# Moving normalizations up the ScalarE queue, turning the first keys early, and mirroring a quarter of the first batch's attention

## The chip, the cores and the metric

The kernel runs on one core of a Trainium2 chip. The metric is the device time of one execution in microseconds (us), less is better. Engines are named as in the profile: PE is TensorE, ACT ScalarE, DVE VectorE, POOL GpSimd, and SP the engine that issues most DMAs. A line number such as L1052 is a line of the kernel before.

## The reference, cut to what matters

There are 16 batches of 1024 rows with 256 features, and per batch a symmetric 0/1 matrix adj of 1024 x 1024. Two layers follow each other; in both the input is normalized, cut at zero and given to a graph block, whose result is added to the input.

```python
# layer 0, for each batch; 8 heads of 32 features
normed = layer_norm(relu(norm(x)), gamma1, beta1)      # queries, keys and values are all this
scores = q @ k.T / sqrt(32); masked where adj == 0; attn = softmax(scores)
h = h + attn @ v
h = h + gelu(layer_norm(h, gamma2, beta2) @ W1 + b1) @ W2 + b2
x = x + h
# layer 1, for each batch
f = relu(norm(x))
logits = (f W a_1).T + f W a_2 + (f W a_12)(f W).T     # leaky relu, mask by adj, softmax
x = x + elu(f @ W_1 + softmax(logits) @ f @ W_2)
```

Queries and keys are one and the same and adj is symmetric, so the matrix of attention weights before the division is symmetric too. What was computed for keys 512 to 1023 against queries 0 to 511 is, turned over, what keys 0 to 511 against queries 512 to 1023 need. The kernel calls that quarter mirrored.

## The kernel before, in words

The program is unrolled over all 16 batches. It is made by several generators (stream_a for attention, stream_b for everything after it, stream_c for the start of a batch, stream_m for masks, stream_p and stream_s for preparations). Each yields a place on a common scale, where b to b+1 is the attention of batch b, and the one with the smallest place goes next. The order in which instructions are made is the order on each engine's queue; the queues are not reordered afterwards. An engine, and SP for its DMAs, works its queue strictly in that order and waits where an operand is missing.

`defer(us, f)` holds f back until an estimated clock has moved on by that much, and `run_deferred` runs what is due. `turns` holds jobs on PE that are let in between two units of attention.

Attention goes by units: one group g of four heads, one half qh of the queries (512) and one tile kt of 128 keys. `scores` (L1016) makes the logits in two PSUM tiles, DVE adds the mask (L1029) and ACT takes the exponential and sums it (L1036, "exps" below); one unit later `weigh` (L1131) multiplies by the values va into o. In batch 0 the first of the two tiles gets its mask on PE instead, by a product with the identity (L574, "s<-mk,ident").

From batch 1 on, the units of qh = 1 with kt below 4 are left out. For each unit of qh = 0 with kt of 4 or more, `mirror` does four things. DVE turns 32 x 32 blocks of the weights into a tile x (L1052, two halves); SP writes x to DRAM in four DMAs (blocks, L1059); POOL adds up x in six operations (add_up, L1065) to row; and SP writes row (L1080). `gather` reads the rows back as sums of the softmax, `fetch` reads blocks back as em (L1099, 512 KB each), and `weigh_mirrored` (L1113) multiplies em by va. The pool of x holds one buffer.

Batch 0 has nothing to run beside its attention: the products of the batch (pty, ph, po, ptf, puT, pg, lg, pa, pf on PE) of batch b run beside the attention of batch b+1, and pty is the first of them. In `prologue(b)`, rows are loaded as h in four chunks, normalized (POOL takes the power -0.5, L745), cut by ACT (L816), normalized again to nrm (DVE, L749), multiplied by gamma (POOL, L829) and increased by beta (L830) to va; PE turns va (ptk, L837) and ACT copies it to kT (L840), the keys. For batch 0 `convert` makes masks of adj and `dma_start_transpose` turns them (mk). For other masks, `turn_masks` loads adj in halves (L587, two buffers), converts them (DVE, L594) and turns them; `compare_masks` checks on POOL (odd, L932) that adj is symmetric.

`normalize_later` takes part in every batch: DVE makes a factor nm (L759) 3.0 estimated us after the statistics, and ACT applies it to y or ft (L765) 5.0 after. y goes to PE as pty, ft as ptf (L1367); ACT copies ptf to fT (L1370), which puT, pg and lg read.

Of the kernel before, what the change touches and what calls it, by code (L numbers as in the profile page):

```python
# [9 lines left out]
F32 = mybir.dt.float32  # L10
# [485 lines left out]
def fast_path(  # L496
# [129 lines left out]
    def weight(src, name, pad=0):  # L626
# [3 lines left out]
        return t  # L630

    g1 = broadcast_row(gamma1, "g1")
    be1 = broadcast_row(beta1, "be1")
    for t, src in rows_to_load:
        nc.scalar.dma_start(t, src)
    rows_to_load.clear()
# [118 lines left out]
    def normalize_later(dst, srcs, stats, name, function):  # L755
        mv, rs = stats
        nm = smallp.tile([P, TPC], F32, tag="nm2", name=f"nm_{name}")
        defer(
            3.0, lambda: nc.vector.scalar_tensor_tensor(nm, mv[:, :, 0], -1.0, rs, op0=ALU.mult, op1=ALU.mult)  # L759
        )  # L760

        def apply():
            t = dst()
            for i, src in enumerate(srcs):
                nc.scalar.activation(t[:, i, :], src, function, bias=nm[:, i : i + 1], scale=rs[:, i : i + 1])  # L765

        return defer(5.0, apply)

# [20 lines left out]
    def prologue(b, st):  # L789
# [33 lines left out]
        def value(i):  # L823
            mv, rs = stats["b", i]
            for j in range(TPC):
                t = i * TPC + j
                nrm = tmpp.tile([P, D], F32, tag="w1", bufs=6, name=f"nrm_{b}_{t}")
                normalize(nrm, h[t // TPH][:, t % TPH, :], mv, rs, j)
                nc.gpsimd.tensor_mul(nrm, nrm, g1)  # L829
                nc.gpsimd.tensor_add(va[:, t, :], nrm, be1)  # L830

        def turn(i):
# [18 lines left out]
        if b == 0:  # L851
# [20 lines left out]
            rectify(0)  # L872
            convert(0)
            rectify(1)
            measure(0, "b")
            convert(1)
            measure(1, "b")
            value(0)
            turn(0)
            convert(2)  # L880
            value(1)
            turn(1)
            convert(3)
# [86 lines left out]

    scored = []

# [17 lines left out]
    def attention(b, st):  # L990
        va, kT = st["va"], st["kT"]
        mirrored = b > 0
        sums = {}
# [6 lines left out]
        def scores(qh, g, kt):  # L1000
# [4 lines left out]

            by_pe = 2 if b == 0 else 0
            if by_pe:
# [37 lines left out]

        def mirror(g, kt, es):
            x = xp.tile([P, NT // 2 * GH, GH, HD], F32, tag="x", name=f"x_{b}_{g}_{kt}")
            if g not in blocks:
# [15 lines left out]
            def add_up():  # L1064
# [30 lines left out]
        def fetch(k):  # L1095
            g, t, half = k // (2 * TPH), k // 2 % TPH, k % 2
            if k == 0:
                blocks["e"] = midp.tile([P, 2, 2 * GH, P], F32, tag="mid0", name=f"em_{b}")
            nc.sync.dma_start(  # L1099
                blocks["e"][:, half],  # L1100
                blocks[g][half * 2 * GH : (half + 1) * 2 * GH, t * GH : (t + 1) * GH].rearrange(
                    "k b i e -> (b i) k e"
                ),
            )

        def weigh_mirrored(k):
            g, t, half = k // (2 * TPH), k // 2 % TPH, k % 2
            e = blocks["e"][:, half]
            if t == half == 0:
# [10 lines left out]
            clock[0] += 0.45  # L1120
            if k + 2 < 2 * TPH * NG:
                defer(0.6, lambda: fetch(k + 2))

        acc, os, rl = {}, {}, {}

        def weigh(qh, g, kt, es, first, last):
            if first and not (mirrored and qh == 1):
                acc[g, qh] = pso.tile([P, QW], F32, tag="o", name=f"o_{b}_{g}_{qh}")
            o = acc[g, qh]
            for j in range(GH):  # L1130
                nc.tensor.matmul(  # L1131
                    o[j * HD : (j + 1) * HD, :],
                    va[:, kt, (g * GH + j) * HD : (g * GH + j + 1) * HD],
                    es[j // 2][:, j % 2, :],
                    start=first and not (mirrored and qh == 1),
                    stop=last,
                )
# [9 lines left out]
        def invert(qh, g):  # L1147
            r = smallp.tile([P, TPH, GH], F32, tag="rl", name=f"rl_{b}_{g}_{qh}")

            def f():  # L1150
                if mirrored and qh == 0:
                    nc.vector.tensor_reduce(
# [9 lines left out]

            rl[g, qh] = r, defer(2.5 if mirrored and qh == 0 else 2.5, f)

        keys = list(range(NT))
        if mirrored:
            keys = [kt for pair in zip(keys[TPH:], keys[:TPH]) for kt in pair]
        units = [(0, g, kt) for g in range(NG) for kt in keys]
        keys = list(range(TPH if mirrored else 0, NT))
        units += [(1, g, kt) for g in range(NG) for kt in keys]  # L1170
        k = 0
        for n, u in enumerate(units):
# [7 lines left out]
            scored.append((weigh, (*u, es, first, last)))  # L1180
            if not mirrored:
                if qh == NQH - 1 and kt % TPH == TPH - 1:
                    invert(kt // TPH, g)
                    if kt < NT - 1:
                        close(kt // TPH, g)
                yield 1.0
                continue
            if qh == 0:
                if kt >= TPH:
                    mirror(g, kt, es)  # L1190
                if n == NG * NT - 3:
                    defer(2.0, lambda: fetch(0))
                    defer(2.2, lambda: fetch(1))
                if n == NT + 1:
                    gather(0)
                if n == NT + 3:
# [374 lines left out]
    def stream_a():  # L1571
        for b in range(B):
            done = 0.0
            yield b
            for width in attention(b, states[b]):
                done += width
                yield b + done / (WIDTH if b else NQH * NG * NT)
        yield from spread(close_attention(), 4, B, B + .1)
# [150 lines left out]
```

## Time and profile before

| | us |
|---|---|
| median of 3 runs | 3367.99 (3364.7 to 3368.45) |
| the profiled execution | 3366.83 |
| its span, first to last instruction | 3365.1 |
| PE busy in the span | 3249.6 (97%) |
| DVE busy | 2688.1 (80%) |
| ACT busy | 2123.7 (63%) |
| POOL busy | 1517.0 (45%) |
| mean granted clock of PE | 0.99 |

Busy time counts every moment in which an engine has an instruction in work. A line of the profile with several groups names the line of the kernel, engine, operation, what is written and read, how often, the busy time, the mean of one in ns, and the idle time ahead of it with what ended it. In a timeline the first number is the start in us from the start of the span, the second the duration; what stands in brackets is the idle time before it and what ended that. "xN" counts the instructions merged into a line.

### The profile page before, as it was taken

To read this page: it belongs to the slowest core of one execution; us is meant where nothing else is said; L and a number is where in the kernel's file an instruction comes from. 1 tells how busy PE (TensorE), PEld (TensorE's weight loads), DVE (VectorE), ACT (ScalarE), POOL (GpSimd) and SP (SyncE) were. 2 spreads that over 40 slices of the span, in tenths; PEclk is the share of its full clock that TensorE was granted. 3 is DMA by queue.
4 is the path that set the end of the run, shared out by engine and by line. 5 is a ranking of instruction groups with operands and counts; after the bars stand their busy time and mean duration, and the time that the engine had idled before them with its cause. 6 is when DMAs were issued, how large, how long until landed. Compare 5 with 4: busy or idle time off the path is not lost. (4 is left out here: it accounts for less than half of the span.)

```text
span 3365.1 us, 114909 instructions
## 1 busy us (share of the span) xinstructions
PE 3249.6 (97%) x48866; PEld 1602.6 (48%) x48866; DVE 2688.1 (80%) x5009; ACT 2123.7 (63%) x5128; POOL 1517.0 (45%) x1757
## 2 busy tenths in 40 slices
PE   6899999999999999999999999999999999999998
PEld 2244445444454544445444454444545444454477
DVE  5788888888888888887888888888888888878734
ACT  6775766757566576665756667576665756657442
POOL 3563553635436264452635536354362644525120
PEclk9999999999999999999999999999999999999999
DMA  5354555545555464554545546455554645553400
GB/s 137 69 123 126 132 124 136 128 123 135 120 133 126 120 138 123 129 123 134 127 126 130 126 134 128 126 131 121 129 125 124 140 116 136 118 136 92 125 30 14
DMA packets 741161, 404.83 MB, mean 120 GB/s; under 512 B 173216, under 2 KB 699936, under 8 KB 740640
## 3 DMA queue, kind: packets, MB, share of 16 engines
q1 hardware_dynamic: 740352, 397.14, 48.0%
q8 instruction: 386, 6.32, 0.8%
q14 instruction: 135, 1.11, 0.1%
q10 hardware_dynamic: 288, 0.26, 0.0%
HBM read 233.97 MB, written 146.54 MB: 113 GB/s over the span
## 5 line engine op out<-in xcount | busy, mean ns | idle before, releaser
L1036 ACT ACTIVATE e<-e 128x512 f32<-128x512 f32 x1504 | 928.3, 618 | 629.2 <-DVE e L1029 626.2
L1029 DVE TENSOR_TENSOR e<-s,mk 128x1024 f32<-128x1024 f32 x752 | 883.9, 1214 | 110.2 <-PE s L1016 100.9
L1016 PE MATMUL s<-kT 32*64 32x512 f32 x6272 | 464.2, 629 | 0.5 <-DVE e L1029 0.5
L574 PE MATMUL ph<-yT,w 128*32 128x256 f32 x7808 | 449.9, 381 | 12.9 <-DVE yT L1298 12.7
L574 PE MATMUL lg<-fT,uT 128*32 128x256 f32 x7680 | 450.3, 379 | 0.3 <-ACT gw L1397 0.3
L574 PE MATMUL pa<-gw,e 128*32 128x258 f32 x7584 | 446.1, 380 | 0.0
L1131 PE MATMUL o<-e,va 128*32 128x512 f32 x3136 | 435.8, 617 | 0.0
L574 PE MATMUL po<-w,hid 128*32 128x256 f32 x7680 | 434.5, 379 | 0.9 <-ACT hid L1326 0.9
L574 PEld LDWEIGHTS ph<-yT,w 128*32 128x32 f32 x7808 | 247.9, 110 | 223.5 <-DVE yT L1298 44.5
L574 PEld LDWEIGHTS po<-w,hid 128*32 128x32 f32 x7680 | 255.1, 110 | 198.6 <-issue 46.1
L574 PEld LDWEIGHTS lg<-fT,uT 128*32 128x32 f32 x7680 | 248.8, 110 | 198.2 <-issue 27.2
L574 PEld LDWEIGHTS pa<-gw,e 128*32 128x32 f32 x7584 | 246.2, 110 | 185.4 <-issue 22.1
L1052 DVE STREAM_TRANSPOSE x<-e 128x1024 f32<-128x1024 f32 x240 | 291.7, 1230 | 39.5 <-ACT e L1036 27.6
L1065 POOL TENSOR_TENSOR part<-part,x 128x512 f32<-128x512 f32 x240 | 311.2, 1297 | 18.8
L1421 ACT ACTIVATE e<-e,shift 128x512 f32<-128x512 f32 x256 | 183.2, 716 | 161.0 <-DVE e L1420 149.7
L1036 ACT ACTIVATION_READ_ACCUMULATOR e<-e 128x1 f32 x1504 | 281.0, 187 | 0.0
L932 POOL TENSOR_TENSOR odd<-mk,mq 128x512 bf16<-128x512 fp8e5 x192 | 219.4, 1160 | 132.2 <-DMA mk<-mq 132.2
L1415 DVE SCALAR_TENSOR_TENSOR e<-lg,gw,mk 128x256 f32<-128x256 f32 x512 | 223.4, 477 | 61.0 <-PE lg L574 49.7
L829 POOL TENSOR_TENSOR nrm<-nrm,g 128x256 f32<-128x256 f32 x128 | 100.5, 785 | 344.2 <-DVE nrm L749 344.2
L1065 POOL TENSOR_TENSOR part<-x 128x512 f32<-128x512 f32 x120 | 157.0, 1308 | 211.9 <-DVE x L1052 206.1
L745 POOL TENSOR_TENSOR rs_c<-ve_c,mhalf 128x2 f32<-128x2 f32 x64 | 44.6, 697 | 428.7 <-DVE ve_c L743 425.1
L1322 ACT ACTIVATE hid<-ph,b1c 128x256 f32<-128x256 f32 x512 | 202.3, 463 | 44.9 <-PE ph L574 30.4
(146 smaller groups left out, 4462.0 us busy)
## 6 DMA issues: line engine op xcount, KB each, us to landing
blocks<-x SPq DMA_DIRECT2D x480, 256.0 KB, 4.6
em<-blocks SPq DMA_DIRECT2D x240, 512.0 KB, 4.3
adj<-in_adj_dram SPq DMA_DIRECT2D x248, 256.0 KB, 3.6
h<-in_x_dram SPq DMA_DIRECT2D x64, 256.0 KB, 4.5
xb<-in_x_dram SPq DMA_DIRECT2D x128, 128.0 KB, 3.8
out_dram<-z SPq DMA_DIRECT2D x128, 128.0 KB, 4.1
rows<-row SPq DMA_DIRECT2D x120, 32.0 KB, 2.4
gather<-rows SPq DMA_DIRECT2D x120, 32.0 KB, 3.7
```

The costliest lines, as they stand in the source:

```text
L574: nc.tensor.matmul(out[c : c + HD], lhsT[:, c : c + HD], rhs, start=start, stop=stop)
L829: nc.gpsimd.tensor_mul(nrm, nrm, g1)
L932: nc.gpsimd.tensor_tensor(odd.rearrange("p (u v x) -> p u v x", u=2, v=2), key.rearrange("p (u v x) -> p u v x", u=2, v=2), query.rearrang ...
L1016: nc.tensor.matmul(sc[j // 2][c : c + P // 2, j % 2, :], kT[r, g, kt * P + c : kt * P + c + P // 2], kT[r, g, qs], start=j >= by_pe, stop= ...
L1029: nc.vector.tensor_tensor(e, masked, mb, op=ALU.add)
L1036: nc.scalar.activation(e[:, j], masked[:, j], AF.Exp, scale=SCALE, accum_out=sums[kt // TPH, g][:, n, kt % TPH, qh : qh + 1],)
L1052: nc.vector.transpose(x[:, :, 2 * i : 2 * i + 2, :].rearrange("p c h j -> p h c j"), es[i].rearrange("p h (c i) -> p h c i", i=HD),)
L1065: add = lambda out, p, q: nc.gpsimd.tensor_tensor(out, p, q, op=ALU.add)
L1131: nc.tensor.matmul(o[j * HD : (j + 1) * HD, :], va[:, kt, (g * GH + j) * HD : (g * GH + j + 1) * HD], es[j // 2][:, j % 2, :], start=first ...
L1322: nc.scalar.activation(hid[:, f0 + i, :], ph[:, i, :], AF.Identity, bias=b1c[:, f0 + i : f0 + i + 1])
L1415: nc.vector.scalar_tensor_tensor(e[:, j, :], lg[:, j, :], gw[:, kt, D : D + 1], st[c // 2][:, kt // 2, qs, kt % 2], op0=ALU.add, op1=ALU.add,)
L1421: ready = defer(2.5, lambda: nc.scalar.activation(e, e, AF.Exp, bias=shift))
```

## The change

`normalize_later` applies the factor 3.1 estimated us after the statistics instead of 5.0, in every batch.

For the first two chunks of batch 0, PE turns nrm itself, ahead of gamma and beta, and ACT applies both on the way to kT, where they are a scale and a bias for each partition (g1c, be1c). POOL makes va of it afterwards. The loads at the start stand in another order, and the parts of the prologue of batch 0 come at earlier places.

Batch 0 gets the mirrored quarter: its units with qh = 1 and kt below 4 are gone, those with qh = 0 and kt of 4 or more are mirrored, and its keys go in the order 0, 1, 4, 2, 5, 3, 6, 7 for the first group of heads and 4, 0, 5, 1, 6, 2, 7, 3 for the second. There em has four halves in two buffers, not two in one. The mask is put on by PE only for qh = 0. Since the estimated clock moves little between two units there, `mirror` runs what is left of the mirror before (mirror_done), and rows and gather are forced ahead too. The masks of batches 0 and 1 are turned at earlier places.

```diff
-        return defer(5.0, apply)
+        return defer(3.1, apply)
...
+                if b == 0 and i < 2:
+                    normed[t] = nrm
+                    continue
                 nc.gpsimd.tensor_mul(nrm, nrm, g1)
                 nc.gpsimd.tensor_add(va[:, t, :], nrm, be1)
+        def turn_normed(i):
...
+                    nc.tensor.transpose(
+                        pt[:, g, j * P : (j + 1) * P], normed[i * TPC + j][:, g * P : (g + 1) * P], ident
+                    )
+            for g in range(NG):
+                nc.scalar.activation(
+                    kT[:, g, i * CW : (i + 1) * CW], pt[:, g, :], AF.Identity, bias=be1c[:, g : g + 1], scale=g1c[:, g : g + 1]
+                )
+            for j in range(TPC):
+                t = i * TPC + j
+                nc.gpsimd.tensor_mul(va[:, t, :], normed[t], g1)
+                nc.gpsimd.tensor_add(va[:, t, :], va[:, t, :], be1)
...
-            for f, i in ((load, 0), (fetch, 0), (load, 1), (fetch, 1), (fetch, 2), (fetch, 3), (load, 2), (load, 3)):
-                f(i)
+            load(0)
+            load(1)
+            for t, src in first_rows:
+                nc.sync.dma_start(t, src)
+            for t in range(TPH):
+                fetch(t)
+            load(2)
+            load(3)
...
-            turn(0)
+            turn_normed(0)
...
-        mirrored = b > 0
+        ahead = 2 if b else 4
...
-            by_pe = 2 if b == 0 else 0
+            by_pe = 2 if b == 0 and qh == 0 else 0
...
         def mirror(g, kt, es):
+            run_deferred(mirror_done[0])
             x = xp.tile([P, NT // 2 * GH, GH, HD], F32, tag="x", name=f"x_{b}_{g}_{kt}")
...
+                mirror_done[1 + g] = clock[0] + 10.0
                 defer(10.0, lambda: nc.sync.dma_start(blocks["rows", g][kt - TPH], row.rearrange("p a t h -> p (a t h)")))
...
-            defer(6.5, add_up)
+            mirror_done[0] = defer(6.5, add_up)
...
-            if k == 0:
-                blocks["e"] = midp.tile([P, 2, 2 * GH, P], F32, tag="mid0", name=f"em_{b}")
+            if k < ahead and k % 2 == 0:
+                tag = "mid0" if b else f"mid{1 + k // 2}"
+                blocks["e", k // 2] = midp.tile([P, 2, 2 * GH, P], F32, tag=tag, name=f"em_{b}_{k // 2}")
...
+        keys = [[kt for pair in zip(range(TPH, NT), range(TPH)) for kt in pair]] * NG
+        if b == 0:
+            keys = [[0, 1, 4, 2, 5, 3, 6, 7], keys[1]]
+        units = [(0, g, kt) for g in range(NG) for kt in keys[g]]
+        units += [(1, g, kt) for g in range(NG) for kt in range(TPH, NT)]
...
                 if n == NG * NT - 3:
-                    defer(2.0, lambda: fetch(0))
-                    defer(2.2, lambda: fetch(1))
-                if n == NT + 1:
+                    for i in range(ahead):
+                        defer(2.0 + 0.2 * i, lambda i=i: fetch(i))
+                late = 0 if b else 2
+                if n == NT + 1 + late:
+                    run_deferred(mirror_done[1])
                     gather(0)
...
             if n == NG * NT + 1:
+                run_deferred(max(mirror_done))
+                run_deferred(max(mirror_done))
                 gather(1)
...
-                for place, _ in zip((0.02, 0.04, 0.07, 0.10, 0.13), prologue(b, states[b])):
+                for place, _ in zip((0.005, 0.01, 0.03, 0.07, 0.13), prologue(b, states[b])):
...
-                start, end = (b - 0.28, b - 0.10) if b == 1 else (b - 0.73, b - 0.60)
+                start, end = (b - 0.55, b - 0.40) if b == 1 else (b - 0.73, b - 0.60)
...
-                yield from spread(compare_masks(b, 0, states[b]), TPH, b + 0.02, b + 0.2)
-                yield from spread(turn_masks(b, 1, states[b]), 5, b + 0.23, b + 0.43)
-                yield from spread(compare_masks(b, 1, states[b]), 2 * TPH, b + 0.52, b + 0.7)
+                yield from spread(compare_masks(b, 0, states[b]), TPH, b + 0.02, b + 0.15)
+                yield from spread(turn_masks(b, 1, states[b]), 5, b + 0.17, b + 0.30)
+                yield from spread(compare_masks(b, 1, states[b]), 2 * TPH, b + 0.32, b + 0.42)
```

More of the change, by code (lines that the diff above doesn't have):

```diff
@@ L630, in weight @@
         return t
+    g1c = columns(gamma1, DC, "g1c")
+    be1c = columns(beta1, DC, "be1c")
+    for t, src in rows_to_load:
+        nc.scalar.dma_start(t, src)
+    rows_to_load.clear()
     g1 = broadcast_row(gamma1, "g1")
     be1 = broadcast_row(beta1, "be1")
-    for t, src in rows_to_load:
-        nc.scalar.dma_start(t, src)
+    first_rows = rows_to_load[:]
     rows_to_load.clear()
@@ L828, in value @@
                 normalize(nrm, h[t // TPH][:, t % TPH, :], mv, rs, j)
+                if b == 0 and i < 2:
+                    normed[t] = nrm
+                    continue
                 nc.gpsimd.tensor_mul(nrm, nrm, g1)
                 nc.gpsimd.tensor_add(va[:, t, :], nrm, be1)
+        normed = {}
+        def turn_normed(i):
+            clock[0] += 0.5
+            pt = ps_tile([P, NG, CW], f"ptk_{b}_{i}")
+            for g in range(NG):
[3 more added lines that the diff above has]
+                    )
+            for g in range(NG):
+                nc.scalar.activation(
+                    kT[:, g, i * CW : (i + 1) * CW], pt[:, g, :], AF.Identity, bias=be1c[:, g : g + 1], scale=g1c[:, g : g + 1]
+                )
+            for j in range(TPC):
+                t = i * TPC + j
+                nc.gpsimd.tensor_mul(va[:, t, :], normed[t], g1)
+                nc.gpsimd.tensor_add(va[:, t, :], va[:, t, :], be1)
         def turn(i):
@@ L872, in prologue @@
             rectify(0)
+            rectify(1)
             convert(0)
-            rectify(1)
             measure(0, "b")
-            convert(1)
             measure(1, "b")
             value(0)
-            turn(0)
+            turn_normed(0)
+            convert(1)
+            value(1)
+            turn_normed(1)
             convert(2)
-            value(1)
-            turn(1)
             convert(3)
@@ L967, in make_turns @@
             f()
-    scored = []
+    scored, mirror_done = [], [0.0, 0.0, 0.0]
     finished = {}
@@ L1096, in fetch @@
             g, t, half = k // (2 * TPH), k // 2 % TPH, k % 2
-            if k == 0:
-                blocks["e"] = midp.tile([P, 2, 2 * GH, P], F32, tag="mid0", name=f"em_{b}")
+            if k < ahead and k % 2 == 0:
+                tag = "mid0" if b else f"mid{1 + k // 2}"
+                blocks["e", k // 2] = midp.tile([P, 2, 2 * GH, P], F32, tag=tag, name=f"em_{b}_{k // 2}")
             nc.sync.dma_start(
-                blocks["e"][:, half],
+                blocks["e", k % ahead // 2][:, half],
                 blocks[g][half * 2 * GH : (half + 1) * 2 * GH, t * GH : (t + 1) * GH].rearrange(
@@ L1107, in weigh_mirrored @@
             g, t, half = k // (2 * TPH), k // 2 % TPH, k % 2
-            e = blocks["e"][:, half]
+            e = blocks["e", k % ahead // 2][:, half]
             if t == half == 0:
@@ L1120, in weigh_mirrored @@
             clock[0] += 0.45
-            if k + 2 < 2 * TPH * NG:
-                defer(0.6, lambda: fetch(k + 2))
+            if k + ahead < 2 * TPH * NG:
+                defer(0.6, lambda: fetch(k + ahead))
         acc, os, rl = {}, {}, {}
         def weigh(qh, g, kt, es, first, last):
-            if first and not (mirrored and qh == 1):
+            if first and qh == 0:
                 acc[g, qh] = pso.tile([P, QW], F32, tag="o", name=f"o_{b}_{g}_{qh}")
@@ L1134, in weigh @@
                     es[j // 2][:, j % 2, :],
-                    start=first and not (mirrored and qh == 1),
+                    start=first and qh == 0,
                     stop=last,
@@ L1150, in f @@
             def f():
-                if mirrored and qh == 0:
+                if qh == 0:
                     nc.vector.tensor_reduce(
@@ L1161, in f @@
                 nc.vector.reciprocal(r, r)
[L1163 to L1170, printed above, removed]
+            rl[g, qh] = r, defer(2.5, f)
+        keys = [[kt for pair in zip(range(TPH, NT), range(TPH)) for kt in pair]] * NG
[3 more added lines that the diff above has]
+        units += [(1, g, kt) for g in range(NG) for kt in range(TPH, NT)]
         k = 0
@@ L1180, in attention @@
             scored.append((weigh, (*u, es, first, last)))
[L1181 to L1187, printed above, removed]
             if qh == 0:
@@ L1191, in attention @@
                 if n == NG * NT - 3:
-                    defer(2.0, lambda: fetch(0))
-                    defer(2.2, lambda: fetch(1))
-                if n == NT + 1:
+                    for i in range(ahead):
[3 more added lines that the diff above has]
+                    run_deferred(mirror_done[1])
                     gather(0)
-                if n == NT + 3:
+                if n == NT + 3 + late:
                     invert(0, 0)
@@ L1576, in stream_a @@
                 done += width
-                yield b + done / (WIDTH if b else NQH * NG * NT)
+                yield b + done / WIDTH
         yield from spread(close_attention(), 4, B, B + .1)
```

## The prediction

> **What bounds the kernel now.** I read the busy time by stretches first: 0 to 20.9 us is the start, up to 138.8 the attention of batch 0 with nothing beside it, 500 to 1000 the repeating middle.
>
> ```profile
> core 0: us, PE busy (x) PEld busy (x) DVE busy (x) ACT busy (x) POOL busy (x), PEclk, DMA share, GB/s
> 0.00:20.90 20.90, 2.65 (x8) 1.36 (x8) 13.17 (x42) 4.25 (x7) 11.68 (x26) 1.00 0.70 194
> 20.90:60.00 39.10, 35.07 (x385) 9.18 (x388) 17.95 (x29) 32.49 (x100) 12.28 (x16) 1.00 0.42 113
> 60.00:100.00 40.00, 34.07 (x460) 10.10 (x453) 29.86 (x62) 32.77 (x104) 16.12 (x19) 1.00 0.30 77
> 100.00:138.80 38.80, 32.44 (x345) 8.65 (x343) 28.98 (x56) 28.71 (x88) 19.70 (x23) 1.00 0.39 83
> 500.00:1000.00 500.00, 491.87 (x7760) 239.84 (x7748) 415.98 (x766) 317.64 (x768) 224.28 (x257) 0.99 0.52 129
> ```
>
> In the middle PE works 98% of the time: there only a PE stall can be won. Batch 0's attention is a loop through PE, ACT and DVE in which none is full: 32 units in 118 us, 3.7 each; the timeline at 69.7, 72.8 and 75.9 has undisturbed units every 3.07. The first PE work of the next phase (pty) starts at 142.0.
>
> Next, PE's waits between 500 and 3100 us:
>
> ```profile
> PE ptf L1367 <- DVE mv_a L741: 21.7, 7, 3.8
> PE ptf L1367 <- ACT ft L765: 13.4, 5, 3.2
> ```
>
> Twelve waits of 2.9 in some 12.7 batches: one a batch, always before ptf. The timeline of one of them:
>
> ```profile
> 2075.79 0.57 ACT L1370 COPY fT<-ptf 128x512 f32<-128x512 f32 x1
> 2078.15 1.90 PE L574 MATMUL puT<-fT,wm 128*32 128x512 f32 x16
> 2082.71 1.07 ACT L765 ACTIVATE ft<-xb,nm_d,rs_d 128x256 f32<-128x256 f32 x2
> 2083.35 0.93 PE L1367 MATMUL ptf<-ident,ft 128*128 128x128 f32 x4 [2.71 <-ACT ft L765]
> ```
>
> ft is late because it stands behind four exps and an odd on ACT, though its factor nm_d was there at 2078.4. 12 of the 14 such stalls (batches 0 to 13) are followed by half a clock for 3.4 us or more (1.7 lost each).
>
> Last, the mirror of the later batches, since batch 0 gets it: its buffer x is single.
>
> ```profile
> blocks<-x SPq DMA_DIRECT2D x480, 256.0 KB, 4.6
> em<-blocks SPq DMA_DIRECT2D x240, 512.0 KB, 4.3
> ```
> ```profile
> 214.64 2.36 DVE L1052 STREAM_TRANSPOSE x<-e 128x1024 f32<-128x1024 f32 x2
> 221.20 3.86 SPq L1059 DMA_DIRECT2D blocks<-x  x4
> 231.28 1.25 DVE L1052 STREAM_TRANSPOSE x<-e 128x1024 f32<-128x1024 f32 x1 [4.36 <-DMA blocks<-x]
> ```
>
> The next turn waits, and all DVE with it, until the four writes have landed. The issues take 3.4 us where nothing holds SP; the last lands 2.6 + 4.6 = 7.2 after the first. Later batches have a mirror each 12 to 17 us, so this rarely shows.
>
> **What the skill says.** "TensorE: Matmul & The Clock Gate", Part 1, has a free-running window of 4096 cycles (3413 ns) that sets full or half rate. The trace agrees: half rate lasts 3.413 or 6.827 us, starts on that grid, and follows windows with 1.70 us idle or more (1.69 and 1.67 did not). "DMA: Bandwidth & Descriptors", Anatomy of one DMA, has semaphores waited for on the issuing sequencer, before dispatch; so a load behind a write that waits for DVE waits too. The trace agrees: SP's L587 waits 286.6 us for DVE's mq. "Perfetto Trace Analysis", Optimization Strategy, reads repeated bubbles as a possible lack of buffers; here the ptf bubble is queue order, the 4.36 above a buffer.
>
> **The change, part by part.** I took the built order of the changed program on each queue and set durations of this trace on it.
>
> *Start.* Both h loads go first, and the keys of chunks 0, 1 are turned from nrm, not from va: eight POOL products and sums (0.79 and 0.75) leave the path. Normalization done near 12.8 instead of 15.4, the last mask transposed near 17 (convert to 14.4, landing 2.5 after issue); first scores at 17 instead of 20.9: -3.9. Two activations a chunk replace one copy (2 x 0.46, from hid's row, for 0.58; beside the mask). It is given back: ptk_2 and ptk_3 now stand before units 1 and 4 and wait for va of chunks 2, 3, behind POOL (eight ops of 0.77, two pows of 0.7). By that walk unit 1 scores at 28.2 (26.2 before), the fourth mask ends near 37.6 (37.2 before). So 0; bounds -4 and +3. The gamma and beta loads moved to SP and ACT lie under the mask loads: 0, bounds 1.
>
> *Mirrored quarter.* Removed: 8 units at 3.07 = 24.6, and the mask by PE in 8 more (0.61 and a 0.42 gap each). Added on PE: 16 weigh_mirrored at 0.62; on DVE: 16 transposes at 1.23 and 8 masks at 1.22; on POOL: 8 add_ups of six ops, 5.3 (1.27 + 2 x 1.29 + 0.73 + 0.45 + 0.31); on SP: 32 writes, 16 em fetches, 8 rows, 8 gathers. The engines' sums allow a gain: DVE's 76.8 in the three stretches grows by 29.4 less 9.8 for the masks of lost units. The chain through x does not. The mirrored key tiles 4 to 7 of head group 0 I call x4 to x7, those of group 1 x14 to x17; each is turned in two halves by DVE. From one's first turn to the next one's:
> - x4 to x5: turn, mask, turn 4.7; adj_4 is behind the four writes on SP and lands 8.8 later, its second half 1.2 later, two converts 0.45; mask 1.2: **16.4**.
> - x5 to x6: adj_5 waits for the two adj buffers (3.6 after a convert): 6 to the second turn; adj_7 behind the writes and a transpose of 1.2, 9.3; two converts, mask: **17.7**.
> - x6 to x7: turns 2.5, writes landed 7.3: **9.9**; x7 to x14 with a mask and os between the turns: **11.8**.
> - x14 to x15: second turn at 5.7 (three reduces); h of batch 1 is loaded behind those writes, landing 9 later; stats 1.4, mask 1.2, reduces 2.7: **19.9**.
> - x15 to x16: second turn at 6.1, adj_1 behind the writes 8.6, converts, mask: **17.0**.
> - x16 to x17: second turn 4.4; adj_3 and four em fetches (1.37 an issue) stand before the writes, 5.8 to their issue, 7.2 to 9 to landing: **19.7**.
>
> Sum 112.4; from 37.6, x17 turns at 150.0. After it: second turn at +6.9, POOL's add_up of x17 behind ten POOL ops at +19.6, rows landed +22, gather issued +24; em of pairs 6, 7 stands behind that gather on SP and lands +30; five units of some 4 us follow, two em buffers sharing (4.3 a fetch and 2.7 issue): PE done at **+51**, 201 against 142.0: **+59**. Each wait has all units queued behind DVE, so none hides. Half clock in the gaps isn't counted (up to +8). Floor of it: seven spacings of 9.9 and 34 after = 141, -1.
>
> *mirror_done.* It only puts add_up, rows and gather earlier in the queues; counted above.
>
> *Apply at 3.1.* In each batch ft_0, ft_2, ft_3 and y_2 move up ACT's queue. ft_2 goes before the fT copy, waits there for nm_d (ACT blocked 2 us; the fT copy behind it, and puT on PE for that). puT then starts 1.75 after nm_d (activations 1.07, copy 0.57): over batches 0 to 13 a stall of 1.5 to 3.3, mean 2.3, for one of 2.95, and ptf takes 0.66, not 0.93: -0.95 a batch, -13. A window catches 1.7 idle in (3.41 - 2.3 + 1.2)/3.41 = 68%, for 12 of 14: -4. ft_0 waits 2 us ahead of the table load of 1.28; the exps start 0.3 later: +4. y_2, ft_3 find their factors ready; the hid and gw drains behind them come 1.1 later, PSUM of 3 covers it: 0, bounds 7 both ways. Sum **-13**, bounds -30 and +10.
>
> *Turning of batch 1's masks earlier* (POOL and SP work) is in the walk. The next phase starts with that work done: **-3**, bounds -8 and +3.
>
> Total 0 + 59 - 13 - 3 = +43 on an execution of 3366.8 (span 3365.1 and 1.7 around it; the median of the runs is 3368.0, 1.2 above): **3410**.
>
> **Rivals.** *A, the forecast:* x's single buffer and SP's order set batch 0's length; 3385 to 3440 with half to all of the extra waits; 0.68. *B, the chain near its floor (faster):* loads behind writes land in their shadow and x turns on the average each 9.9; -1 - 13 - 3 gives 3350. With 34 after, the total is 7 spacings - 86.4 against before (37.6 + 34 - 142.0 - 16): faster by 7 or more below 11.3 us a spacing. For it: engines' sums have room. Against it: only two of seven spacings in the order have no load or late stats between. 0.13. *C, half of the loads hidden:* spacing 12.5, 40 after: 165 against 142, less 16, +7: 3374; 0.12. *D, the exchange on ACT loses too:* clock halved in each batch still and exps late, ft_2 at +0.7 a batch: 59 + 10 - 3: 3433; 0.07. That the change doesn't do what it says is excluded by the built order. POOL as the bound: its 36 us from 42 to 138.8 and 42 of add_ups make 78, less than the 97 there.
>
> **Numbers.** 3410; from B's edge to D: 3358 to 3440. About 0.2% (7 us) can be told from no change. Faster: most of B, 0.13; within: 0.07; slower: 0.80.
>
> **What would show it.** In the changed profile: DVE's x turns waiting for blocks<-x and adj in batch 0, spacings of 10 to 20, pty near 200; one puT wait of some 2.3 a batch on fT in place of ptf's. Wrong if pty comes before 160, or DVE's waits for writes sum to under 20 us there; or if ptf still waits 3 us in the middle.

## The result, and the profile after

| | before | after |
|---|---|---|
| median of 4 runs each, us | 3368.22 | 3414.00 |
| ratio to before | | 1.013 [1.011, 1.015] |
| the profiled execution, us | 3366.83 | 3415.79 |
| its span, us | 3365.1 | 3414.0 |
| pty of batch 0 starts at, us | 142.0 | 209.6 |
| from there to the end of the span, us | 3223.1 | 3204.4 |

The change made the kernel slower by 46 us in the medians and by 49 in the profiled executions. The last two rows split that: batch 0's attention became 67.6 us longer, and all that follows became 18.7 us shorter. These two rows come from one execution of each kernel; the executions of the kernel before spread from 3359.6 to 3377.5 us, so a few us in them are not to be read. Line numbers are from here on those of the kernel that is shown; in the changed kernel L1085 turns x, L1092 writes blocks, L1148 is weigh_mirrored, L1061 adds the mask, L594 converts later masks, L744 takes the statistics of h, L763 makes nm, L769 applies, L1401 copies fT, L1428 gw.

Busy time by stretches in the changed kernel, with the columns of the table before. The fourth stretch runs to pty and is longer than before's.

```profile
20.90:60.00 39.10, 21.70 (x208) 5.25 (x208) 15.85 (x32) 19.40 (x58) 19.39 (x24) 0.86 0.52 131
60.00:100.00 40.00, 23.61 (x260) 7.13 (x260) 14.47 (x17) 12.32 (x42) 15.49 (x17) 0.71 0.62 131
100.00:138.80 38.80, 18.45 (x124) 4.20 (x124) 23.52 (x42) 12.95 (x39) 21.82 (x25) 0.68 0.54 126
138.80:209.60 70.80, 44.95 (x404) 13.86 (x400) 45.42 (x83) 33.13 (x100) 35.51 (x42) 0.79 0.74 183
500.00:1000.00 500.00, 487.86 (x7628) 236.74 (x7620) 421.83 (x790) 316.95 (x771) 237.91 (x274) 1.00 0.53 127
```

Read the first number in each group. Between 60 and 100 us PE is busy for 23.6 where it was 34.1, DVE for 14.5 where it was 29.9, ACT for 12.3 where it was 32.8; only POOL, which got the sums of x, has nearly as much to do as before. No engine is near full, so the question is what they wait for. DVE's longest waits for transfers, first in the kernel before up to 150 us, then in the changed one up to 220:

```profile
DVE mq L594 <- DMA adj<-in_adj_dram: 6.5, 6, 1.7
...
DVE st_a L740 <- DMA h<-in_x_dram: 3.6, 2, 2.0
```
```profile
DVE mq L594 <- DMA adj<-in_adj_dram: 26.1, 7, 9.2
DVE x L1085 <- DMA blocks<-x: 22.2, 3, 7.7
...
DVE st_a L744 <- DMA h<-in_x_dram: 9.1, 2, 7.2
```

The numbers are the sum in us, how often, and the longest. The three of the changed kernel make 57.4 us; before, the two make 10.1, and there are no writes of x to wait for. One such wait in the timeline, between the mirrors of x4 and x5: SP issues four writes from 48.80 and only then the adj loads, and DVE, which has the mask of the next unit queued behind the convert, stands for 9.15 us.

```profile
48.80 3.40 SPq L1092 DMA_DIRECT2D blocks<-x  x4
...
52.24 6.98 SPq L587 DMA_DIRECT2D adj<-in_adj_dram  x4
...
57.93 0.94 DVE L594 TENSOR_SCALAR mq<-adj 128x512 fp8e5<-128x512 int32 x2 [9.15 <-DMA adj<-in_adj_dram]
58.79 1.22 DVE L1061 TENSOR_TENSOR e<-s,mk 128x1024 f32<-128x1024 f32 x1
...
59.92 1.23 DVE L1085 STREAM_TRANSPOSE x<-e 128x1024 f32<-128x1024 f32 x1
```

In the middle (500 to 3100 us) PE's wait ahead of ptf is gone, and others stand in its place:

```profile
PE puT L574 <- ACT fT L1401: 22.1, 13, 3.1
PE pg L574 <- ACT gw L1428: 6.3, 12, 0.5
PE pg L574 <- ACT fT L1401: 6.1, 12, 0.5
```

In the timeline the order on ACT has turned round: ft now stands ahead of the copy to fT, both wait for nm_d, and puT waits for the copy.

```profile
2135.58 1.10 DVE L763 SCALAR_TENSOR_TENSOR nm_d<-mv_d,rs_d 128x2 f32<-128x2 f32 x1 [0.99 <-POOL rs_d L749]
...
2136.72 1.09 ACT L769 ACTIVATE ft<-xb,nm_d,rs_d 128x256 f32<-128x256 f32 x2 [1.71 <-DVE nm_d L763]
2137.72 0.56 ACT L1401 COPY fT<-ptf 128x512 f32<-128x512 f32 x1
...
2138.33 1.50 PE L574 MATMUL puT<-fT,wm 128*32 128x512 f32 x12 [1.74 <-ACT fT L1401]
```

Of the windows of half rate between 500 and 3100 us, 11 of 3.41 us in the kernel before, one is left.

### The profile page after: what moved, and what is told of

Same layout as the page of the kernel before. It is cut to its first block, busy times and chain, and to the rows that moved or that the text cites. A ratio compares the mean times of both kernels' runs of the same rounds, so it can differ in the third digit from the quotient of the medians.

```text
span 3414.0 us, 114649 instructions
## 1 busy us (share of the span) xinstructions
PE 3246.3 (95%) x48674; PEld 1610.6 (47%) x48674; DVE 2716.3 (80%) x5027; ACT 2110.7 (62%) x5066; POOL 1558.4 (46%) x1805
## 5 line engine op out<-in xcount | busy, mean ns | idle before, releaser
L1061 DVE TENSOR_TENSOR e<-s,mk 128x1024 f32<-128x1024 f32 x752 | 883.0, 1214 | 94.3 <-PE s L1048 89.0
L574 PE MATMUL ph<-yT,w 128*32 128x256 f32 x7808 | 454.9, 381 | 11.5 <-DVE yT L1329 11.4
L1166 PE MATMUL o<-e,va 128*32 128x512 f32 x3072 | 428.7, 613 | 0.0
L574 PEld LDWEIGHTS ph<-yT,w 128*32 128x32 f32 x7808 | 263.9, 110 | 206.1 <-DVE yT L1329 42.4
L1085 DVE STREAM_TRANSPOSE x<-e 128x1024 f32<-128x1024 f32 x256 | 311.4, 1230 | 54.1 <-ACT e L1068 27.3
L1098 POOL TENSOR_TENSOR part<-part,x 128x512 f32<-128x512 f32 x256 | 332.1, 1297 | 20.1
L574 PEld LDWEIGHTS pa<-gw,e 128*32 128x32 f32 x7584 | 246.2, 110 | 185.3 <-issue 22.1
L1098 POOL TENSOR_TENSOR part<-x 128x512 f32<-128x512 f32 x128 | 167.0, 1305 | 250.0 <-DVE x L1085 244.2
```

The source lines that it names most:

```text
L574: nc.tensor.matmul(out[c : c + HD], lhsT[:, c : c + HD], rhs, start=start, stop=stop)
L1061: nc.vector.tensor_tensor(e, masked, mb, op=ALU.add)
L1085: nc.vector.transpose(x[:, :, 2 * i : 2 * i + 2, :].rearrange("p c h j -> p h c j"), es[i].rearrange("p h (c i) -> p h c i", i=HD),)
L1098: add = lambda out, p, q: nc.gpsimd.tensor_tensor(out, p, q, op=ALU.add)
L1166: nc.tensor.matmul(o[j * HD : (j + 1) * HD, :], va[:, kt, (g * GH + j) * HD : (g * GH + j + 1) * HD], es[j // 2][:, j % 2, :], start=first ...
```

## The experiments

Each was timed against the kernel before on the same chip. The last column counts windows of half rate, 3.41 us each, between 500 and 3100 us in the trace's record of the granted clock. It and the two columns ahead of it are of the profiled execution alone. Where an expectation speaks of 12 windows in the middle of the kernel before, this count has 11.

| run | median us | before beside it | ratio to before | pty at | pty to end | half rate |
|---|---|---|---|---|---|---|
| apply_alone | 3353.3 | 3365.1 | 0.9964 [0.9949, 0.9978] | 142.7 | 3210.5 | 2 |
| all_but_apply | 3424.6 | 3365.1 | 1.0169 [1.0154, 1.0183] | 207.3 | 3215.8 | 11 |
| start_alone | 3369.8 | 3365.1 | 1.0013 [1.0006, 1.0020] | 147.1 | 3223.4 | 11 |
| start_late_turns_apply | 3353.3 | 3365.1 | 0.9968 [0.9957, 0.9980] | 141.2 | 3208.8 | 0 |
| x_twice | 3402.8 | 3365.6 | 1.0113 [1.0097, 1.0128] | 198.9 | 3201.8 | 1 |
| masks_loaded_ahead | 3393.3 | 3365.6 | 1.0085 [1.0070, 1.0100] | 192.0 | 3200.1 | 0 |
| both_ahead | 3384.8 | 3365.6 | 1.0061 [1.0046, 1.0076] | 181.5 | 3200.9 | 0 |
| h_and_rows_ahead | 3375.2 | 3366.2 | 1.0023 [1.0016, 1.0030] | 170.8 | 3206.0 | 3 |
| checks_late | 3380.4 | 3366.2 | 1.0038 [1.0024, 1.0052] | 174.9 | 3204.5 | 3 |
| stall_filled | 3346.7 | 3365.6 | 0.9952 [0.9938, 0.9965] | 142.4 | 3202.0 | 1 |
| stall_part_filled | 3362.9 | 3367.7 | 0.9985 [0.9978, 0.9992] | 143.1 | 3217.8 | 8 |
| start_late_turns_filled | 3346.3 | 3366.2 | 0.9936 [0.9922, 0.9951] | 145.4 | 3199.3 | 0 |

**The apply step, alone and left out.**

```diff
 # apply_alone, on the kernel before
-        return defer(5.0, apply)
+        return defer(3.1, apply)
 # all_but_apply, on the kernel after
-        return defer(3.1, apply)
+        return defer(5.0, apply)
```

> The kernel before with one edit: the apply step held back 3.1 estimated us, not 5.0. Theory (the gain of the change outside batch 0 is all the apply step's): the later batches of the changed kernel were 18.7 us shorter than before, so 13 to 20 us faster than before, 3348 to 3355, with the ptf waits gone, puT waits of some 1.8 on fT, and most of the half-rate windows of the middle gone. Rival (the gain came from batch 1's masks being done earlier, the apply step is worth nothing): within 4 us of before. Rival D of the prediction (the exchange on ACT loses): 3 to 10 us slower than before. In either case pty stays within 2 us of 142.

> The changed kernel with the apply step put back to 5.0. Theory: the later batches get their ptf waits and their half-rate windows back, 13 to 20 us slower than the changed kernel, 3427 to 3434, pty within 3 us of 209.6. Rival (the apply step is worth nothing): within 4 us of 3414. Rival (the two parts act on each other, as when apply at 3.1 lengthens batch 0 itself): pty comes more than 4 us earlier.

Alone it brought 11.9 us in the medians, 12.6 from pty to the end; left out it cost 10.6 in the medians, 11.4 from pty to the end. It hardly touches batch 0: pty moved by 0.7 and by 2.3. Both are short of the 13 to 20 us expected, so a part of the 18.7 us is not its own: all_but_apply is still 7.3 us shorter after pty than before (see the next phase, below).

**The start alone, and with the late turns.** Start_alone takes the diff's turn_normed, order of loads and places of the prologue. The other keeps before's places and has the apply step at 3.1:

```diff
-                for place, _ in zip((0.005, 0.01, 0.03, 0.07, 0.13), prologue(b, states[b])):
+                for place, _ in zip((0.02, 0.04, 0.07, 0.10, 0.13), prologue(b, states[b])):
```

> The kernel before with the start of the change alone: keys of chunks 0 and 1 turned from nrm with gamma and beta as scale and bias, the order of the loads, and the earlier places in the prologue, so that ptk_2 stands ahead of unit 1 and ptk_3 ahead of unit 3. Neither the mirrored quarter nor the apply step at 3.1. The prediction took 0 for it (bounds -4 and +3). Theory from the changed trace (first scores at 22.0 where 20.9 were before, unit 1 at 33.0 where it was at 25.3): the start loses 4 to 7 us, pty at 146 to 149 and 3371 to 3375 in all. Rival (that delay belongs to the mirrored quarter's key order and not to the start): within 2 us of before.

> The kernel before with the apply step at 3.1 and with the turned keys and load order of the change, but ptk_2 and ptk_3 left at their old places, so that unit 1 need not wait for them. Theory (early ptk_2 is what costs at the start, the earlier keys themselves bring 0 to 3 us): 0 to 3 us faster than the kernel with the apply step alone, 3346 to 3354, pty at 139 to 143. Rival (the late first mask transpose, which landed 4.1 us after PE was free, and POOL's products behind it cost on their own): 1 to 5 us slower than the apply step alone.

The start lost 4.6 us in the medians (2 to 7 by the interval) and 5.1 at pty. Here is PE in start_alone:

```profile
21.20 1.04 PE L574 MATMUL s<-mk,ident 128*32 128x512 fp8e5 x8 [4.06 <-DMA mk<-mq]
...
29.81 0.47 PE L863 MATMUL ptk<-ident,va 128*128 128x128 f32 x1 [5.62 <-POOL va L837]
...
32.12 1.04 PE L574 MATMUL s<-mk,ident 128*32 128x512 fp8e5 x8
```

PE has turned the first keys by 17.1, but stands 4.1 us for the mask, and then 5.6 for va of chunk 2 ahead of the second unit, at 32.12. With the late turns PE stands 4.1 us for the mask as well, but the first scores start at 20.50 (20.93 before) and the second unit at 24.84 (25.27 before), pty is at 141.2, and the time equals that of the apply step alone. So what the start loses comes from ptk_2 ahead of the second unit; and the turned keys by themselves bring nothing that can be measured, since the mask comes no earlier. Why the mask is late shows on SP in the changed kernel:

```profile
1.67 0.42 SPq L897 DMA_DIRECT2D g<-in_L_gnn_gamma_dram  x1
2.14 0.43 SPq L897 DMA_DIRECT2D be<-in_L_gnn_beta_dram  x1
2.61 4.01 SPq L886 DMA_DIRECT2D adj<-in_adj_dram  x4
...
11.72 8.97 SPq L892 DMA_TRANSPOSE mk<-mq  x4
```

The four mask transposes take 9.0 us of SP in either kernel. They began at 8.71 before and begin at 11.72 here, since the first adj load stands behind the second h load, gamma and beta, and its convert waits for it until 10.99. In start_alone and with the late turns, which have the same order of loads, they begin at 10.88 and 10.17: the order costs 1.5 to 3.0 us in the chain that decides when the first scores start. No run says how much of that is the h load's and how much gamma's and beta's.

**A second buffer for x, and the mask loads out of the way.**

```diff
 # x_twice
+            second = b == 0 and kt % 2 == 1
-            x = xp.tile(..., tag="x", ...)
+            x = (midp if second else xp).tile(..., tag="mid0" if second else "x", ...)
 # masks_loaded_ahead: 512 KB loads into buffers that are free
             convert(3)
+            ahead_of(0, 1, range(TPH, NT), ("mid2", "mid1"))
...
                 yield from spread(turn_masks(b, 1, states[b]), 5, b + 0.17, b + 0.30)
+                ahead_of(1, 0, range(TPH - 1), ("mid2",))
```

ahead_of loads the rows of adj that are named into the buffers that are named, and turn_masks takes them from there. Both_ahead has both edits, with x's second buffer as here.

> The changed kernel with a second buffer for x in batch 0 (every other mirror takes a buffer that is free until batch 0's products). Nothing else moves. Theory (x's single buffer and SP's order set batch 0 together): the 22 us that DVE waits for blocks<-x go, but loads still stand behind the writes, so waits for adj and h (35 us) stay or grow: pty 195 to 205, 5 to 15 us faster than the changed kernel, 3399 to 3409. Rival (x's buffer alone is the cause): 22 to 45 us faster, adj waits shrink too. Rival (PE's half clock, DVE or POOL as the bound): within 3 us of 3414.

> The changed kernel with the adj loads of the mirror stretch taken from behind the writes on SP: adj_4 to adj_7 are loaded at the start into two buffers that are free then, adj_0 to adj_2 of batch 1 ahead of the writes of x7; adj_3 and the h loads stay. x stays single. Theory: DVE's 26 us of waits for adj nearly go, waits for blocks<-x take part of their place (floor of 9.9 a mirror): pty 175 to 190, 20 to 35 us faster than the changed kernel, 3379 to 3394. Rival (x's buffer alone is the cause): blocks<-x takes the whole place, within 6 us of 3414. Rival (PE's half clock, DVE or POOL as the bound): within 3 us.

> Both: x twice in batch 0 and the adj loads ahead of the writes. Theory: what is left is adj_3, the h loads (9 us), POOL's add_up and the end after x17; mirrors come every 7 to 9 us: pty 150 to 170, 40 to 60 us faster than the changed kernel, 3354 to 3374, so about where the kernel with the apply step alone was (3353) and not clearly below it. Rival (the engines bound the stretch: DVE 106 us, POOL 78): no more than 10 us faster than the better of the two parts. Rival (the mirrored quarter wins once its loads are out of the way): below 3346.

Against the changed kernel's 3414.0 these are 11, 21 and 29 us less (9, 18 and 27 if each is set against the kernel before that ran beside it). What DVE waits for up to 220 us, first with x twice, then with the masks ahead:

```profile
DVE mq L594 <- DMA adj<-in_adj_dram: 28.9, 9, 8.9
...
DVE x L1086 <- DMA blocks<-x: 3.7, 1, 3.7
```
```profile
DVE x L1104 <- DMA blocks<-x: 27.5, 5, 7.6
...
DVE mq L594 <- DMA adj<-in_adj_dram: 4.2, 3, 2.6
```

Each edit takes its own wait and leaves or raises the other. So neither the buffer nor the queue order alone is the cause: it takes both, as the prediction had it. Both together fell short of the 40 to 60 us that were expected. By its numbers the rival of the engines holds (8.5 us better than the better part), but the trace has another reason for at least a part:

```profile
76.67 2.08 SPq L1134 DMA_DIRECT2D rows<-row  x1
...
81.72 0.30 POOL L1118 TENSOR_TENSOR row<-part 128x64 f32<-128x64 f32 x1 [7.35 <-DMA rows<-row]
81.98 3.36 POOL L983 TENSOR_TENSOR odd<-mk,mq 128x512 bf16<-128x512 fp8e5 x3
83.16 0.69 DVE L995 TENSOR_REDUCE uneven<-odd 128x1 f32<-128x512 bf16 x1 [9.36 <-POOL odd L983]
```

A small write of rows stood behind the four writes of x7 on SP. Its buffer (there are two) came free late, POOL stood for it 7.35 us, the check odd stood behind POOL's sum, and DVE's reduce behind odd for 9.36, with the transposes of x queued behind that. So at least this wait is the same queue again, through two more engines.

**What was left in the way.** In the first, h of batch 1 is loaded at the start and rows are written earlier; the second has the masks and checks at the places of the kernel before.

```diff
 # h_and_rows_ahead, on both_ahead
+            take_h(1)
+            for i in range(NCH):
+                load_h(1, i)
...
-                mirror_done[1 + g] = clock[0] + 10.0
-                defer(10.0, lambda: nc.sync.dma_start(blocks["rows", g]...
+                held = 10.0 if b else 5.0
+                mirror_done[1 + g] = clock[0] + held
+                defer(held, lambda: nc.sync.dma_start(blocks["rows", g]...
 # checks_late, on both_ahead, whose loads for batch 1 it drops
-                start, end = (b - 0.55, b - 0.40) if b == 1 else ...
+                start, end = (b - 0.28, b - 0.10) if b == 1 else ...
...
-                yield from spread(compare_masks(b, 1, states[b]), 2 * TPH, b + 0.32, b + 0.42)
+                yield from spread(compare_masks(b, 1, states[b]), 2 * TPH, b + 0.52, b + 0.7)
```

> Both parts (x twice, adj loads ahead) and two more: all h loads of batch 1 go to the start, ahead of every write, and in batch 0 rows are written 5 estimated us after add_up and not 10, so ahead of the next mirror's writes. In the trace with both parts DVE waited 9.9 us for h, and 9.4 us for a check on POOL that stood behind a row buffer which its write to DRAM had not freed for 7.4 us. Theory (the queue order on SP is what lengthens the stretch, wait after wait): pty at 162 to 172, 10 to 18 us faster than with both, 3367 to 3375; still above the kernel with the apply step alone. Rival (POOL and DVE work is the rest, not the queue): within 4 us of 3385. Rival B of the prediction (the mirrored quarter wins once the waits are gone): below 3353.

> x twice, adj_4 to adj_7 at the start, and the masks and checks of batches 0 and 1 at the places of the kernel before (the checks of keys 4 to 7 at 0.52 to 0.70 of the phase, batch 1's masks at 0.72 to 0.90), so that POOL's checks and DVE's reduces stand behind the mirrors. Theory (checks behind a late row hold DVE for 9 us in the stretch of the mirrors, but batch 1's adj loads now stand among the em fetches): 0 to 10 us faster than with both parts, 3375 to 3385. Rival (em fetches behind adj loads, which wait for converts, lengthen the end by more): 5 to 20 us slower than with both parts. Rival (POOL's checks cost nothing): the mirrors keep their spacing of 12.

They brought 9.7 and 4.4 us over both_ahead; the first is just short of the 10 to 18 expected. With the checks late the mirrors come each 10.4 us (x4 turns at 43.8, x17 at 116.4) where both_ahead has 12.0, so the checks in the stretch did cost; but from x17 to pty it takes 58.6 us where both_ahead takes 55.4. With h and rows ahead the first turn of x4 is at 42.6 and that of x17 at 121.1, 11.2 us a mirror where the changed kernel has 16.2. DVE is busy 64.6 us of these 78.5: most of the waits are gone, and the stretch nears its engines. But the end after x17 hardly shrank:

```profile
42.60:121.10 78.50, 54.98 (x544) 15.40 (x543) 64.63 (x95) 40.48 (x129) 55.02 (x62) 0.82 0.74 168
121.10:170.80 49.70, 35.27 (x320) 11.96 (x320) 30.82 (x53) 24.97 (x76) 23.80 (x28) 0.77 0.70 174
```
```profile
144.22 1.08 PE L1181 MATMUL o<-em,va 128*32 128x256 f32 x8 [5.76 <-DMA em<-blocks]
145.98 1.08 PE L1181 MATMUL o<-em,va 128*32 128x256 f32 x8 [0.68 <-DMA em<-blocks]
```

It takes 49.7 us against 52.7 in the changed kernel, with a fetch of em still awaited for 5.8; no run takes this end apart. So even with four causes out of the way the kernel with the mirrored quarter is at 3375.2, some 21 us above the one with the apply step alone, each set against the kernel before beside it. Of these the start is some 5.

**PE's wait filled.** Twelve, and then five, transposes of the identity are put ahead of ptf_2 in the kernel before. They write into its tile and are overwritten; nothing waits for them.

```diff
             pt = ps_tile([P, DC, CW], f"ptf_{b}_{c}")
+            for i in range(12 if c == 2 and b < B - 1 else 0):
+                nc.tensor.transpose(pt[:, 0, :P], ident, ident)
```

> The kernel before (apply step at 5.0) with twelve idle-time transposes of the identity (0.165 each, 2.0 us) into the tile of ptf_2 ahead of the real ones, batches 0 to 14: PE does them while it waits for ft_2. No other edit. Theory (half of what the apply step brought is the clock: each half-rate window costs some 1.5 us of PE time, and it comes from idle time of 1.7 us or more in one window of 3.41): stall of 1 us left, half-rate windows in the middle 0 to 3 instead of 12, 12 to 20 us faster than before, 3345 to 3353. Rival (the half-rate windows cost nothing in the end, or follow no idle): within 3 us of before. Rival (the filling makes ptf late): slower than before.

> As the kernel with PE's wait filled, but with five transposes (0.8 us) in place of twelve, so that some 2.1 us of the 2.95 are left idle. In all the traces so far every window of 3.41 us with 2.1 us idle or more was followed by half rate and none with 1.65 or less. Theory (the idle time within one window decides, and each half-rate window costs 1.7 us): 3 to 8 of the middle's 12 half-rate windows are left, 7 to 14 us faster than before, between the kernel before and the filled one. Rival (any work in the wait is enough, whatever its length): as the filled one, 3344 to 3350. Rival (the gain comes from something else than the clock): half-rate windows and gain do not go together.

> The kernel before with the apply step left at 5.0, the twelve transposes in PE's wait for ft_2, and the turned keys and load order of the change with ptk_2 and ptk_3 at their old places. Theory: the parts add, 0 to 3 us for the start on top of the filled kernel's 19: 3344 to 3348, faster than both kernels of the case. Rival (the start shifts the waits against the window of the clock and the half rate comes back): 3350 to 3362.

```profile
2071.11 1.53 PE L1366 MATMUL ptf<-ident 128*128 128x128 f32 x12 [0.92 <-DVE xb L1346]
...
2072.43 1.08 ACT L765 ACTIVATE ft<-xb,nm_d,rs_d 128x256 f32<-128x256 f32 x2
...
2073.08 0.93 PE L1369 MATMUL ptf<-ident,ft 128*128 128x128 f32 x4 [0.44 <-ACT ft L765]
```

ft comes no earlier than it did (it starts 4.9 us after nm_d does, and so it did in the batch that the prediction shows); PE only has something to do meanwhile. Of the 11 windows of half rate one is left, and the kernel is 18.9 us faster in the medians (12 to 21 by the interval of the ratio). That is more than the 11.9 of the apply step, though the intervals of the two ratios overlap; with the turned keys beside each they do not (0.9936 against 0.9968). The edit adds nothing but PE work, so the gain is put down to the clock. Two batches of the kernel before show the price of a window, the first without one, the second with one:

```profile
1166.42:1368.60 202.18, 199.00 (x3138) 96.69 (x3137) 171.92 (x315) 131.24 (x317) 98.19 (x114) 1.00 0.53 129
1368.60:1573.66 205.06, 200.61 (x3140) 98.31 (x3138) 170.31 (x315) 131.33 (x317) 97.50 (x113) 0.99 0.52 128
```

The same number of matmuls, but for two, takes PE 1.61 us more. The other batches agree. Of the 14 from the second pty to the last (348 to 3206 us) ten have one such window, and PE is busy for 200.3 to 200.7 us in them; two with as many matmuls have none, and it is 199.0 and 199.1. So a window costs 1.5 us on the mean. With the stall filled 11 of the 12 windows in these 14 batches went, 16 us at that price, and the 14 became 18.2 us shorter. The kernel before shows the price with no edit at all: its executions beside the experiments took 3362.7 us on the mean where the granted clock reads 0.992 (21 of 89), 3366.5 at 0.991 (41), 3369.8 at 0.990 (23) and 3371.8 at 0.989 (4). A step of 0.001 is 3.4 us of full rate lost, two windows, and goes with 3.0 us, so most of the spread of this kernel goes with its clock. With five transposes 8 windows were left, as the expectation allowed, and the gain was 4.8 us, short of the 7 expected, as three windows fewer would give. Start_late_turns_filled shows the start's parts worth nothing on top (3346.3 against 3346.7, intervals that overlap; its pty came 3.0 us later and the rest was 2.7 shorter, each in one execution). Stall_filled and start_late_turns_filled are faster than both kernels of the case.

## Why the prediction was right, point by point

**The sum.** It said +43 on the execution and 3410; +49 and 3414.0 came. The forecast's mechanism holds: undoing the queue order and the buffer, one by one, brought the ratio to before from 1.013 to 1.0023. That the sum came so near is in part luck: batch 0 was forecast 8.6 us too short (67.6 for 59) and the rest 2.7 too long (-18.7 for -16), and inside the terms there are errors that cancel.

**Start: 0 said (bounds -4 and +3), +5.1 measured.** Two steps failed. "The gamma and beta loads ... lie under the mask loads: 0" did not hold, because they and the second h load were put ahead of them on SP: the transposes began 3.0 us later than before, and the first scores came at 22.0, not at 17. That took away the gain of 3.9, but did not make the loss, as the late turns with the same loads lose nothing. The loss is the second step: unit 1, walked at 28.2, came at 33.0, as ptk_2 waits for va of chunk 2 (5.6 us there), which POOL makes later than walked.

**Mirrored quarter: +59 said, +62.5 measured** (pty of the changed kernel less that of start_alone). The walk's spacings can be laid beside those of the trace:

| from, to | walked | trace |
|---|---|---|
| x4, x5 | 16.4 | 16.5 |
| x5, x6 | 17.7 | 19.2 |
| x6, x7 | 9.9 | 10.0 |
| x7, x14 | 11.8 | 11.5 |
| x14, x15 | 19.9 | 19.0 |
| x15, x16 | 17.0 | 17.1 |
| x16, x17 | 19.7 | 20.2 |
| x17 to PE done | 51 | 49.3 |

The sum of the seven is 113.5 for 112.4. The first turn came at 43.4, not at 37.6; that is mostly the start's error carried on. One slip is in the +59 itself: it sets the walk's 201, where PE is done with batch 0's attention, against 142.0, where pty starts before. PE is done at 138.8 there, and pty waits another 3.2 for y (3.4 in the changed kernel). Like set against like, the walk said +62, and +62.5 came. The walk held because each term was a queue read off in its order with a duration of the trace of before. But its single terms held less well than the spacings: from x16 to x17 the second turn came 3.1 after the first (4.4 said) and the writes were issued 9.2 after that (5.8 said), and the terms written down for it make at most 19.2, where 19.7 was set. So a part of the agreement is luck. The half rate that it left out (PE's clock is 0.68 to 0.86 in the stretch) was inside the waits or small; no run here separates it.

**Apply: -13 said, -11 to -13 measured, but of other parts.** Between 500 and 3100 us PE's listed waits make 50.8 us before and 46.6 with the apply step alone: 0.33 a batch, 5 us over 14 batches, where the stall was to give 13, less 4 for ft_0. The waits of pg on gw and fT, 10.3 us there and none listed before, are what the line "the hid and gw drains ... PSUM of 3 covers it: 0" missed. The clock was to give 4 and gave more: from the second pty to the last 10 of the 12 windows went, 15 us at 1.5 each. Against these 20 stands PE's busy time in a batch without half rate, 199.6 with the edit where it was 199.0, some 8 us over 14 batches. That leaves 12, and these 14 batches became 10.2 us shorter; why PE is busy longer is not settled. So the total of -13 is luck: two terms missed by far and in opposite ways. The estimate that a window would still catch enough idle time in 68% of the batches was the failing step. The stall that it was made from, 2.3, came out at 1.7 (22.1 / 13), for which the same formula gives 50%; but only 2 of the 14 batches had a window of half rate, so the threshold of 1.70 in it was wrong too (see the last section).

**Next phase: -3 said (to -8), 0 to be seen.** From pty to the end all_but_apply is 7.3 us shorter than before, but not where the earlier masks could show: from the first pty to the second it takes 205.9 us in both. Of the 7.3, 5.3 lie in the 14 batches after that and 1.9 in the last. What is left of the edit there is mirror_done, and the prediction read it too narrowly: in the later batches it puts the four writes of one mirror ahead of the gather on SP, where they stood behind it (in one batch gather at 1243.3 and writes at 1245.4 before, writes at 1309.1 and gather at 1313.1 in all_but_apply). No run has it alone, so whether the 5.3 are its doing or the spread between executions stays open.

**Rivals.** C needs a mirror each 12.5 us, and the changed kernel has one each 16.2. B was worked out with 34 us after x17. With the waits taken away the spacing fell to 11.2, under its point of 11.3, and the kernel still lost: the end stays near 50, and with 50 the point lies 16/7 lower, at 9.0, and lower still with the first turn at 42.6, not 37.6. D fell: the exchange on ACT gains. POOL as the bound was rightly at no cost in the changed kernel. In both_ahead DVE does wait 9.4 us for POOL, but POOL itself stood for a write; by busy time DVE is nearer to its bound with the waits gone (64.6 of 78.5 us, POOL 55.0).

## What to carry to other kernels

Read the queue that issues the transfers as an engine of its own: a load behind a write waits for whatever the write waits for, and taking such waits away one at a time hands the time on to the next until the engines themselves are met. Before moving work off PE in a stretch where no engine is full, count what each removed unit costs there and what every added transfer stands behind. A short, regular stall can cost half as much again through the clock (here 2.9 us of waiting and 1.5 of half rate a batch); putting work that nobody needs into it is a cheap test, and here it made the fastest kernels.

## What the runs showed of the hardware that was not expected

**Idle time in one window does not alone decide the half rate.** "TensorE: Matmul & The Clock Gate" of the Trainium skill, Part 1, has the free-running window of 4096 cycles, and half rate after one idle window of about 3.4 us. The grid of 3.413 us held in all runs; but the windows ahead of half rate were seldom wholly idle, most only for 2 to 3 us, so half rate comes sooner here than the page has it. The prediction's reading, half rate after 1.70 us idle in one window, did not hold: laid on that grid, the busy records of PE show windows with 2.05 us idle that were not followed by half rate (h_and_rows_ahead, near 472 us; one with 1.75 near 111 us in the kernel before), and with five transposes in the stall windows with 1.43 and 1.48 that were. From 250 us on, in the runs without added transposes, none with 1.65 or less was followed by it, and all with 2.1 or more were; in batch 0 windows with 1.3 and 1.4 were followed (both_ahead and h_and_rows_ahead, near 59 and 72 us). Records of matmuls have modelled ends, so what the clock counts may be something other than this idle time; what it is stays open. Nor is the record of the clock complete: the same eight products with the mask take 1.04 us at 20.9 and 25.3 us in the kernel before and 0.61 from 29.7, though the record has no half rate until 142.

**Batches can lock to the window.** A batch of the kernel before takes 204.4 to 205.5 us in most cases, and 60 windows make 204.8, so its stall falls at nearly the same place of a window each time: the half rate came every 204.8 us from 449 to 1064 and from 1470 to 2289, and in start_alone eleven times from 862 to 2910. The half rate helps to make that length itself, as the two batches without it took 202.2 and 202.5. With the stall filled or the apply step earlier most batches take 202 to 204, and the pattern is gone. That the length is the reason is argued from these numbers; no run sets it by itself.
